# One written order over the whole kernel, a first chunk in halves, and key subtraction one step ahead

## The chip, the cores and the metric

The kernel runs on one core of one Trainium2 chip. A core has five engines that run beside each other, each with its own instruction queue taken in order: TensorE (PE in the profile, with its weight loads shown as PEld), VectorE (DVE), ScalarE (ACT), GpSimd (POOL) and SyncE (SP), which here issues all the transfers. The metric is the device time of one execution in microseconds (us); lower is better.

## What is computed

One transformer layer in float32, on x of shape 2 x 2048 x 256: attention with compressed queries and keys and rotary parts, then a gated feed-forward part.

```python
h = layernorm(x)
kv_c = h @ W_kv;  kv_c = kv_c * rsqrt(mean(kv_c * kv_c) + 1e-6) * g_kv     # 256 -> 64
q_c = h @ W_q                                                               # 256 -> 128
k = concat(heads(kv_c @ W_kdec, 16), rope(heads(h @ W_krope, 32)))          # 16 heads of 48
q = concat(heads(q_c @ W_qdec, 16), rope(heads(q_c @ W_qrope, 32)))
v = heads(kv_c @ W_vdec, 16)
x = x + (softmax(causal(q @ k.T / sqrt(48))) @ v) @ W_o
h = layernorm(x)
x = x + (silu(h @ Wg.T) * (h @ Wu.T)) @ Wd.T      # integer weights times 1/127, hidden size 768
```

## The kernel before

**Tiling.** Each batch of 2048 tokens is cut in four chunks of 512 (`CH`), so there are eight chunks or groups `(b, g)`. The 16 heads are taken four at a time (`u` from 0 to 3). A step of the attention is `(b, u, g)`: four heads, one chunk of queries, all chunks of keys up to `g`. There are 32 steps.

**Part 1, projections.** For each chunk a chain of jobs runs: `measure` (layer-norm moments on DVE, the inverse root on POOL), `norm` (scaling on DVE), `turn` (eight PE transposes and one ACT copy to `xln`), `compressed` (the `kvq` matmuls, L252 and L255, then ACT copies to `qc` and `kv` and a mean of squares on DVE and POOL), `kv_norm` (ACT), `kv_turn` (PE transposes, ACT). Then `project_jobs` makes keys and queries: `k_0`, `k_1` (`rp_k`, L298, eight PE instructions each) and `q_0`, `q_1` (`rp_q`, L301); each is followed by two DVE multiplications from PSUM with the cosine and sine tables (`tcos`, `tsin`, L306), two POOL additions (L308, L309) and a store to DRAM. `q_content`, `k_content` and `v` follow (L319, L335) with ACT copies. All PSUM tiles of this part come from one ring of four, `two`. The chains of chunks `i+1` and `i+2` are woven between the projections of chunk `i`. The `tcos` tiles are a ring of three, and the raw weights `w_kr_raw` (two) and `w_qh_raw` are staged in that same ring first; `rope_columns` picks columns out of them on ACT.

**Part 2, attention.** Keys and queries are loaded back by head (`load_k`, four steps ahead; `load_q`, two steps ahead). `from_first` subtracts the first key of the batch from all keys, in place, on DVE (L140, L141). In each step, for each 128 keys, `st` matmuls (L535) give scores, ACT takes the exponential (L540), POOL clears the masked triangle in the step's own last chunk (L547), and `acc` matmuls (L561) sum the values, one chunk of keys late. The `st` tiles are a ring of three (`big`). `loads(i)` at the head of a step also issues slices of other work: weight pieces of the feed-forward part, and for the first groups `packed` (loads of attention output and sums), `inverted` (reciprocal on DVE, and a way through DRAM) and `divided`. A table `early` puts the first groups' `projected`, `added`, `measured`, `normed` and `normalized` between the last steps.

**Part 3, feed-forward.** For each group, six times `hidden` (`gu` matmuls, L692, then silu on ACT, a product on DVE, and a split in two halves on ACT and POOL), and between them jobs of the groups that follow: `measured`, `divided`, `packed` after the first, `finished` (L720) of the group before, `normed`, `inverted`, `projected` (`ps_o`, L459) and `added` (L465) after the second, `normalized` (`tp_f`, L499 to L501) and the load of x after the fourth. The `gu`, `ps_o`, `tp_f` and `d` tiles share the ring `big`.

**Order.** Each of the three parts stands in its own block of `tc.manual_schedule(engines=order)`: inside it every engine runs its instructions in the order in which they are written. On an engine, an instruction that waits holds all that are written behind it.

Of the kernel before, what the change touches and what calls it, by code (L numbers as in the profile page):

```python
# [9 lines left out]
FP = mybir.dt.float32  # L10
# [8 lines left out]
P = 128  # L19
# [21 lines left out]
def block_kernel(ctx: ExitStack, tc: tile.TileContext, x, w_kv, g_kv, w_kc, w_v, w_q, w_qh, w_kr, w_o,  # L41
# [25 lines left out]
    def inverse_sqrt(dst, src, eps):  # L67

        nc.gpsimd.tensor_scalar_add(dst, src, eps)
        nc.gpsimd.tensor_tensor(dst, dst, neg_half, ALU.pow)  # L70

    def moments(src, name):

        stats = small.tile([P, NT, 6], FP, tag="stats", name=f"stats_{name}")
        mv = small.tile([P, NT, 2], FP, tag="mv", name=f"mv_{name}")
        rstd = small.tile([P, NT], FP, tag="rstd", name=f"rstd_{name}")
        for t in range(NT):
            nc.vector.bn_stats(out=stats[:, t, :], in_=src[:, t, :])
        for t in range(NT):
            nc.vector.bn_aggr(out=mv[:, t, :], in_=stats[:, t, :])  # L80
        inverse_sqrt(rstd, mv[:, :, 1], LN_EPS)
        return mv, rstd

    def scaled(dst, src, mv, rstd):
        for t in range(NT):
# [61 lines left out]


    with ExitStack() as actx:
# [8 lines left out]
        actx.enter_context(tc.manual_schedule(engines=order))  # L158
        xt = {(0, 0): load_x(prep, 0, 0, bufs=3)}
# [6 lines left out]
        def staged(src, shape, name):  # L166
            w = rope.tile(shape, FP, tag="tcos" if shape[0] == P else "done", bufs=3 if shape[0] == P else 2, name=name)
# [3 lines left out]
        w_kr_raw = [staged(w_kr[d * P:(d + 1) * P, :], [P, NH * 64], f"w_kr_raw_{d}") for d in range(2)]  # L171
        w_kv_sb = weight(w_kv, [P, 2, KVR], "w_kv_sb", True)
        w_q_sb = weight(w_q, [P, 2, QR], "w_q_sb", True)

# [42 lines left out]
        for d in range(2):  # L217
            rope_columns(w_kr_sb[:, d, :], w_kr_raw[d])
# [66 lines left out]
        def project_jobs(b, g):  # L285
# [3 lines left out]
            def rope_job(e, k):  # L289

                def job():
# [11 lines left out]
                    tcos = rope.tile([P, 2, CH], FP, tag="tcos", bufs=3, name=f"tcos_{name}")  # L303
# [51 lines left out]
        for k in (measure, norm, turn):  # L355
            job(0, k)
        job(1, measure)

        first_loads = ([(load_k, step) for step in steps[:NC]] + [(load_q, step) for step in steps[:AHEAD]]
                       + [(from_first, step) for step in steps[:NC]])  # L360
# [6 lines left out]
        for i, one in enumerate(chunks):  # L367
# [3 lines left out]
            k_0()  # L371
            if i == 0:

                job(1, norm)
                columns()
                job(0, compressed)
                k_1()
                job(1, turn)
                job(0, kv_norm)
                job(2, measure)  # L380
                q_0()
                job(0, kv_turn)
                q_1()
                job(1, compressed)
            else:
                job(i + 2, measure)
# [99 lines left out]
    def normed(b, g):  # L486

        of, xns[b, g] = xns[b, g], taken([P, NT, C], FP, tag="xn", name=f"xn_f_{b}_{g}")
        scaled(xns[b, g], x1[b, g], *of)
# [14 lines left out]
    with ExitStack() as actx:  # L504
# [76 lines left out]
        def loads(i):  # L581
# [13 lines left out]
            if 0 <= j < 3:  # L595
# [34 lines left out]
        with tc.manual_schedule(engines=order):  # L630

            end = len(steps) - 1
            early = {(end - 2, 1, 0): (projected, added), (end - 2, 1, 2): (measured,), (end - 1, 0, 2): (normed,),
                     (end - 1, 1, 0): (normalized,), (end - 1, 2, 0): (projected, added)}
            waiting = []
            for i, step in enumerate(steps):
                loads(i)
                by_chunk = exp_jobs(*step)
                for c, (jobs, values) in enumerate(by_chunk):
                    for k, job in enumerate(jobs):  # L640
                        job()
                        if k == 0 and waiting:
                            waiting.pop()()
                        if c == 0 and k == 3 and NC - 1 < i + NC - 1 < len(steps):
                            from_first(*steps[i + NC - 1])
                        if k in (0, 2):
                            for one in early.get((i, c, k), ()):
                                one(*groups[0 if i < len(steps) - 2 or c < 2 else 1])
                    waiting.append(values)
            waiting.pop()()  # L650
# [83 lines left out]
    with tc.manual_schedule(engines=order):  # L734
        x1[groups[2]] = load_x(fp, *groups[2], bufs=4)
        for i, one in enumerate(groups):
            parts[one] = split("hT_%d_%d" % one, [P, NF, CH])
            for f in range(NF):
                hidden(*one, f)
                if f == 0:  # L740
                    if i + 1 < len(groups):
                        measured(*groups[i + 1])
                    if 2 < i + 2 < len(groups):
                        divided(*groups[i + 2])
                    if i + 3 < len(groups):
                        packed(*groups[i + 3])
                if f == 1:
                    if i:
                        finished(*groups[i - 1])
                    if i + 1 < len(groups):  # L750
                        normed(*groups[i + 1])
                    if i + 3 < len(groups):
                        inverted(*groups[i + 3])
                    if i + 2 < len(groups):
                        projected(*groups[i + 2])
                        added(*groups[i + 2])
                if f == 3:
# [204 lines left out]
```

## Time and profile before

| what | value |
|---|---|
| median of 3 runs | 1095.1 us (1094.64 to 1097.89) |
| the profiled execution's own time | 1096.71 us |
| its span, first to last instruction | 1095.0 us |
| PE busy | 1066.9 us (97%), 6657 matmul instructions |
| ACT busy | 654.5 us (60%) |
| DVE busy | 310.0 us (28%) |
| POOL busy | 281.2 us (26%) |
| moved by DMA | 93.25 MB, mean 85 GB/s |

Part 1 takes the first 177 us of the span, attention the stretch from 177 to 922 us, and the feed-forward part the rest. A busy time is a sum over the whole span, while each part has its own limits. The granted clock of PE is listed by stretch: 1.00 is full speed and 0.50 is half. The float32 matmuls appear as two PE instructions each. Spans in the tables are in us from the first instruction; in a row of groups the time in square brackets is the engine's idle time just before, with what ended it.

### The profile page before, as it was taken

The numbers are of one execution on the slowest core, as the hardware profiler recorded it, in microseconds if no ns is written. First come the engines' busy times: TensorE is split into PE (matmuls) and PEld (weight loads), VectorE is DVE, ScalarE is ACT, GpSimd is POOL, SyncE is SP. The second block draws the span as 40 slices with busy tenths as digits, with TensorE's granted clock in tenths as the row PEclk, the third lists the DMA queues.
The fourth block names the chain that finished last, engine by engine and source line by source line (L and its number), as shares of the span: only waits on it lengthen the run. The fifth ranks groups of instructions, "written<-read, shape, count | busy, mean of one in ns | idle before, by whom it ended". The sixth has DMA issues, their size and how long they took to land.

```text
span 1095.0 us, 16796 instructions
## 1 busy us (share of the span) xinstructions
PE 1066.9 (97%) x6657; PEld 536.8 (49%) x6657; DVE 310.0 (28%) x454; ACT 654.5 (60%) x816; POOL 281.2 (26%) x377
## 2 busy tenths in 40 slices
PE   6999998999999999999999999999999999899997
PEld 3455544444433433444344344444435445788886
DVE  4677793200210210120011121003001101656552
ACT  2343344777777677777777767767776675343242
POOL 2666764111110210211121031021111001455343
PEclk9999999999999999999999999999999999999999
DMA  8556746110610421311031033122101001242201
GB/s 192 167 210 203 251 139 217 56 39 23 182 55 13 135 75 61 92 54 39 20 104 53 31 98 98 40 78 80 39 14 36 11 10 43 89 131 87 79 20 43
DMA packets 54440, 93.25 MB, mean 85 GB/s; under 512 B 9296, under 2 KB 22992, under 8 KB 54352
## 3 DMA queue, kind: packets, MB, share of 16 engines
q1 hardware_dynamic: 54352, 92.09, 27.3%
q8 instruction: 54, 0.88, 0.4%
q14 instruction: 34, 0.28, 0.1%
HBM read 49.09 MB, written 42.98 MB: 84 GB/s over the span
## 4 chain that ended last, share of the span: by engine, by line
PE 91%; DMA 4%; POOL 2%; DVE 1%; SPq 1%; issue 1%; ACT 0%; DVEq 0%; ACTq 0%; POOLq 0%
PE st L535 45%; PE acc L561 22%; PE gu L692 8%; PE d L720 4%; PE rp_k L298 3%; PE ps_o L459 3%; PE rp_q L301 2%; DMA x<-in_x_dram 2%; DMA kc<-cont_k 1%; DMA w_qh_raw<-in_w_qh_dram 1%; PE kvq L255 1%; PE kvq L252 1%; PE tp_f L499 1%; PE cp_q L319 1%; PE cp_k L319 1%
## 5 line engine op out<-in xcount | busy, mean ns | idle before, releaser
L540 ACT ACTIVATE es<-st 128x1024 f32<-128x1024 f32 (+1 forms) x576 | 513.2, 995 | 172.4 <-PE st L535 171.8
L535 PE MATMUL st<-qT,kT 48*128 48x512 f32 (+3 forms) x2560 | 496.8, 537 | 3.5 <-issue 3.0
L535 PEld LDWEIGHTS st<-qT,kT 48*128 48x128 f32 x2560 | 228.6, 186 | 251.2 <-ACT es L540 117.8
L547 POOL TENSOR_SCALAR_AFFINE_SELECT es<-es 128x256 f32<-128x256 f32 (+1 forms) x192 | 96.3, 510 | 644.2 <-ACT es L540 644.0
L561 PE MATMUL acc<-es,v_sb 128*32 128x512 f32 (+3 forms) x2560 | 250.5, 531 | 0.0
L561 PEld LDWEIGHTS acc<-es,v_sb 128*32 128x32 f32 x2560 | 74.8, 109 | 183.5 <-issue 145.4
L141 DVE TENSOR_TENSOR kT<-kT,k 48x1024 f32<-48x1024 f32 x64 | 81.8, 1279 | 155.1 <-DMA kT<-kc 108.4
L695 ACT ACTIVATE silu<-gu 128x512 f32<-128x512 f32 x48 | 28.6, 598 | 94.3 <-PE gu L692 94.3
L704 POOL TENSOR_TENSOR hT_lo<-h,hT_hi 128x512 fp32r<-128x512 f32 x48 | 61.7, 1287 | 77.3 <-ACT hT_hi L703 77.3
L298 PE MATMUL rp_k<-xln,w_kr_sb 128*128 128x512 f32 x128 | 61.1, 622 | 1.1 <-ACT xln L98 1.1
L699 DVE SCALAR_TENSOR_TENSOR h<-gu,silu 128x512 f32<-128x512 f32 x48 | 33.0, 689 | 83.8 <-ACT silu L695 58.5
L720 PE MATMUL d<-w_d,hT_lo 128*128 128x256 f32 x192 | 46.4, 283 | 0.0
L720 PE MATMUL d<-w_d,hT_hi 128*128 128x256 f32 x192 | 46.4, 283 | 0.0
L569 ACT COPY at<-acc 128x512 f32<-128x512 f32 x32 | 18.7, 585 | 38.9 <-PE acc L561 35.3
L692 PE MATMUL gu<-x_f_hi,w_g 128*128 128x512 f32 x96 | 40.0, 417 | 0.2 <-DVE h L699 0.2
L298 PEld LDWEIGHTS rp_k<-xln,w_kr_sb 128*128 128x128 f32 x128 | 24.2, 198 | 29.4 <-issue 27.6
L692 PE MATMUL gu<-x_f_lo,w_g 128*128 128x512 f32 x96 | 38.0, 396 | 0.0
L692 PE MATMUL gu<-x_f_hi,w_u 128*128 128x512 f32 x96 | 37.6, 392 | 0.0
L692 PE MATMUL gu<-x_f_lo,w_u 128*128 128x512 f32 x96 | 37.4, 390 | 0.0
L720 PEld LDWEIGHTS d<-w_d,hT_lo 128*128 128x128 f32 x192 | 36.8, 192 | 0.3
L720 PEld LDWEIGHTS d<-w_d,hT_hi 128*128 128x128 f32 x192 | 36.8, 192 | 0.3
L258 ACT COPY qc<-kvq 128x512 f32<-128x512 f32 x8 | 4.7, 586 | 44.5 <-PE kvq L255 44.5
(94 smaller groups left out, 744.1 us busy)
## 6 DMA issues: line engine op xcount, KB each, us to landing
x<-in_x_dram SPq DMA_DIRECT2D x16, 512.0 KB
kr<-tcos_k SPq DMA_DIRECT2D x16, 512.0 KB
qr<-tcos_q SPq DMA_DIRECT2D x16, 512.0 KB
kT<-kr SPq DMA_DIRECT2D x64, 128.0 KB
qT<-qr SPq DMA_DIRECT2D x64, 128.0 KB
ad<-at SPq DMA_DIRECT2D x32, 256.0 KB
vd<-v_sb SPq DMA_DIRECT2D x8, 574.0 KB
qc<-cont_q SPq DMA_DIRECT2D x8, 512.0 KB
```

The costliest lines, as they stand in the source:

```text
L141: nc.vector.tensor_tensor(t[rows], t[rows], k0[b, u][rows].unsqueeze(2).to_broadcast([DIM, 2, CH]), ALU.subtract)
L298: nc.tensor.matmul(ps[:, s, :], lhsT=w_kr_sb[:, d, cols], rhs=xln[b, g][:, d, :], start=(d == 0), stop=(d == 1))
L459: nc.tensor.matmul(ps[:, t * C:(t + 1) * C], lhsT=attn[b, g][:, d, t * P:(t + 1) * P], rhs=w_o_sb[:, d, :], start=(d == 0), stop=(d == 1))
L535: nc.tensor.matmul(ps[:, a, i * w:(i + 1) * w], lhsT=kT[b, u, c][rows, r, j * P:(j + 1) * P], rhs=qT[b, u, g][rows, r, off:], start=True, ...
L540: nc.scalar.activation(e[:, :, :used], ps[:, :, :used], AF.Exp, scale=SCALE)
L547: nc.gpsimd.affine_select(out=block, in_=block, compare_op=ALU.is_ge, fill=0.0, base=0, pattern=pattern, channel_multiplier=-1)
L561: nc.tensor.matmul(acc[b, u, g][r0:r0 + 32, off:], lhsT=vv[b, c][:, j, h * VW:h * VW + 32], rhs=es[kt, p][:, a], start=(kt == 0), stop=(kt ...
L692: nc.tensor.matmul(ps[:, k, :], lhsT=w[:, d, cols], rhs=x2[b, g][s][:, d, :], start=(d == 0 and s == 0), stop=(d == 1 and s == 1))
L695: nc.scalar.activation(s, ps[:, 0, :], AF.Silu, scale=WS)
L699: nc.vector.scalar_tensor_tensor(h, ps[:, 1, :], WS, s, ALU.mult, ALU.mult)
L704: nc.gpsimd.tensor_tensor(lo, h, hi.bitcast(FP), ALU.subtract)
L720: nc.tensor.matmul(ps[t], lhsT=parts[b, g][s][:, f, t * P:(t + 1) * P], rhs=w_d[:, f, :], start=(f == 0 and s == 0), stop=(f == NF - 1 and ...
```

## The change

**Order.** One block of `manual_schedule` (`written`) covers all three parts, from the first load to the last store, in place of three.

**Start.** x of the first chunk comes in two loads of two tiles each. Moments, scaling, transposes and copies of the first chunk are done by halves (moments of both halves, then scaling of both). `w_kv` and `w_q` are loaded ahead of `w_kr_raw`, the `tcos` ring has four buffers, and `rope_columns` of `w_kr` stands behind the copies of `xln`. PE transposes the identity 26 times before the first chunk's transposes, and four times after them, into a PSUM tile `warm` that nobody reads; it is the first of the ring `two`. In chunk 0 the jobs run in the order `compressed(0)`, `k_0`, `measure(1)`, `columns`, `k_1`, `norm(1)`, `kv_norm(0)`, `q_0`, `kv_turn(0)`, `q_1`, `measure(2)`, `turn(1)`, `compressed(1)`.

**Subtraction.** Part 1 holds `from_first` of step 0 alone, one place later than before; each step of the attention then has `from_first` of the next step behind its second tile of keys. Before, the first four stood in part 1 and each step had that of the third step ahead behind its fourth tile.

**Before the feed-forward part.** `packed` of group 3 moves to step 27 of the attention, `measured` and `normed` of group 1 to the last step (with a tile of its own in `xpool`), and in part 3 `packed` runs four groups ahead instead of three.

The diff, without the lines that only move to the left with the blocks:

```diff
-        actx.enter_context(tc.manual_schedule(engines=order))
-        xt = {(0, 0): load_x(prep, 0, 0, bufs=3)}
+        written.enter_context(tc.manual_schedule(engines=order))
+        xt = {(0, 0): prep.tile([P, NT, C], FP, tag="x", bufs=3, name="x_0_0")}
+        halves = [slice(i * NT // 2, (i + 1) * NT // 2) for i in range(2)]
+        for half in halves:
+            nc.sync.dma_start(out=xt[0, 0][:, half],
+                              in_=x[0, half.start * P:half.stop * P, :].rearrange("(t p) d -> p t d", p=P))
...
-            w = rope.tile(shape, FP, tag="tcos" if shape[0] == P else "done", bufs=3 if shape[0] == P else 2, name=name)
+            w = rope.tile(shape, FP, tag="tcos" if shape[0] == P else "done", bufs=4 if shape[0] == P else 2, name=name)
...
-        w_kr_raw = [staged(w_kr[d * P:(d + 1) * P, :], [P, NH * 64], f"w_kr_raw_{d}") for d in range(2)]
         w_kv_sb = weight(w_kv, [P, 2, KVR], "w_kv_sb", True)
         w_q_sb = weight(w_q, [P, 2, QR], "w_q_sb", True)
+        w_kr_raw = [staged(w_kr[d * P:(d + 1) * P, :], [P, NH * 64], f"w_kr_raw_{d}") for d in range(2)]
...
-        for k in (measure, norm, turn):
-            job(0, k)
-        job(1, measure)
+        warm = two("warm")
+        def turn_unit(times):
+            for _ in range(times):
+                nc.tensor.transpose(warm[:, 0, :P], ident, ident)
+
+        turn_unit(26)
+        xn = prep.tile([P, NT, C], FP, tag="xn", name="xn_0_0")
+        xln[0, 0] = prep.tile([P, 2, CH], FP, tag="xln", name="xln_0_0")
+        of = [moments(xt[0, 0][:, half], f"0_0_{i}") for i, half in enumerate(halves)]
+        tp = two("tp_0_0")
+        for half, one in zip(halves, of):
+            scaled(xn[:, half], xt[0, 0][:, half], *one)
+        for half in halves:
+            for t in range(half.start, half.stop):
+                for d in range(2):
+                    nc.tensor.transpose(tp[:, d, t * P:(t + 1) * P], xn[:, t, d * P:(d + 1) * P], ident)
+            cols = slice(half.start * P, half.stop * P)
+            nc.scalar.copy(xln[0, 0][:, :, cols], tp[:, :, cols])
+        turn_unit(4)
+        for d in range(2):
+            rope_columns(w_kr_sb[:, d, :], w_kr_raw[d])
 
         first_loads = ([(load_k, step) for step in steps[:NC]] + [(load_q, step) for step in steps[:AHEAD]]
-                       + [(from_first, step) for step in steps[:NC]])
+                       + 2 * [(lambda *step: None, steps[0])] + [(from_first, steps[0])])
...
-            k_0()
             if i == 0:
-                job(1, norm)
-                columns()
-                job(0, compressed)
-                k_1()
-                job(1, turn)
+                job(0, compressed)
+                k_0()
+                job(1, measure)
+                columns()
+                k_1()
+                job(1, norm)
                 job(0, kv_norm)
-                job(2, measure)
                 q_0()
                 job(0, kv_turn)
                 q_1()
+                job(2, measure)
+                job(1, turn)
                 job(1, compressed)
             else:
+                k_0()
...
-            if 0 <= j < 3:
+            if 0 <= j < 3 or (j, k) == (3, 0):
                 (packed, inverted, divided)[k](0, j)
...
-            early = {(end - 2, 1, 0): (projected, added), (end - 2, 1, 2): (measured,), (end - 1, 0, 2): (normed,),
-                     (end - 1, 1, 0): (normalized,), (end - 1, 2, 0): (projected, added)}
+        early = {(end - 2, 1, 0): ((projected, 0), (added, 0)), (end - 2, 1, 2): ((measured, 0),),
+                 (end - 1, 0, 2): ((normed, 0),), (end - 1, 1, 0): ((normalized, 0),),
+                 (end - 1, 2, 0): ((projected, 1), (added, 1)), (end, 0, 2): ((measured, 1),),
+                 (end, 1, 2): ((normed, 1),)}
...
-                        if c == 0 and k == 3 and NC - 1 < i + NC - 1 < len(steps):
-                            from_first(*steps[i + NC - 1])
+                    if c == 0 and k == 1 and i + 1 < len(steps):
+                        from_first(*steps[i + 1])
...
-                    if i + 1 < len(groups):
-                        measured(*groups[i + 1])
+                if 0 < i < len(groups) - 1:
+                    measured(*groups[i + 1])
...
-                    if i + 3 < len(groups):
-                        packed(*groups[i + 3])
+                if i + 4 < len(groups):
+                    packed(*groups[i + 4])
...
-                    if i + 1 < len(groups):
-                        normed(*groups[i + 1])
+                if 0 < i < len(groups) - 1:
+                    normed(*groups[i + 1])
...
+    written.close()
```

`moments` and `scaled` take the number of tiles from their source instead of always four; nothing else in them changes.

## The prediction

> **What bounds the kernel now.** I read the page's busy times and its chain first, then PE's waits, then the granted clock by stretch, then the timeline at each place where PE waits. The page:
>
> ```profile
> PE 1066.9 (97%) x6657; PEld 536.8 (49%) x6657; DVE 310.0 (28%) x454; ACT 654.5 (60%) x816; POOL 281.2 (26%) x377
> ...
> PE 91%; DMA 4%; POOL 2%; DVE 1%; SPq 1%; issue 1%; ACT 0%; DVEq 0%; ACTq 0%; POOLq 0%
> ```
>
> PE ends the chain nearly everywhere, and from 180 to 830 us it is busy 100% of every stretch at clock 1.00. The change takes no matmul out and adds 30 transposes, so time can only come from PE's idle 28 us and from what PE does at half clock. The waits of PE (engine, line, who released it: us in total, times, longest):
>
> ```profile
> PE tp L97 <- DVE xn L86: 9.0, 1, 9.0
> PE st L535 <- issue: 3.0, 1, 3.0
> PE tp_f L499 <- DVE x L465: 2.8, 1, 2.8
> PE cp_k L319 <- DVE tsin_q L306: 2.7, 1, 2.7
> PE ktp L279 <- ACT kvn L272: 1.6, 1, 1.6
> PE rp_k L298 <- ACT xln L98: 1.1, 1, 1.1
> ```
>
> Each occurs once: at the start (9.0, 1.1), in chunk 0 (2.7), at the end of the projections (1.6), at the first score (3.0), in the first feed-forward group (2.8). The last 7 us after PE's end are untouched. Now the clock, in stretches of 3.41 us (columns: busy us of PE, PEld, DVE, ACT, POOL, then PEclk, DMA share, GB/s):
>
> ```profile
> 38.33:41.74 3.41, 2.88 (x10) 1.83 (x12) 3.41 (x6) 0.77 (x1) 2.89 (x3) 0.50 0.02 5
> ...
> 161.20:164.62 3.42, 2.16 (x7) 1.16 (x8) 3.18 (x3) 1.97 (x5) 3.19 (x3) 1.00 0.61 211
> 174.87:178.28 3.41, 1.05 (x5) 0.85 (x7) 2.25 (x2) 0.59 (x1) 1.08 (x1) 1.00 0.58 202
> 178.28:181.70 3.42, 3.42 (x13) 2.70 (x11) 0.00 (x0) 2.25 (x3) 2.35 (x6) 0.50 0.36 139
> ...
> 936.06:939.47 3.41, 3.41 (x13) 3.00 (x12) 1.68 (x3) 1.64 (x2) 1.27 (x1) 0.50 0.27 95
> 11.03:14.44 3.41, 2.31 (x5) 0.97 (x4) 0.00 (x0) 1.01 (x1) 0.00 (x0) 1.00 0.96 188
> ```
>
> The clock falls to 0.50 for exactly one such stretch after each long wait, and all edges lie on one grid of 3.41 us. A stretch with 1.05 us of PE work was followed by a slow one, one with 2.16 us was not. At the start the column says 1.00, but the eight `rp_k` instructions took 6.21 us there (12.44 to 18.65) against 3.43 later (22.16 to 25.59): PE began slow, stayed so after a stretch with 2.31 us of work, and ran fast from 17.85, after a full one. The three later slow stretches cost half of their PE time: 1.44, 1.71 and 1.70 us.
>
> What ends the three middle waits, from the timeline (start, duration, engine):
>
> ```profile
> 34.79 1.40 DVE L78 BATCH_NORM_STATS2 stats<-x 128x6 f32<-128x256 f32 x4 [6.64 <-DMA x<-in_x_dram]
> ...
> 174.77 1.22 DVE L306 TENSOR_TENSOR tcos_q<-rp_q,cos 128x1024 f32<-128x1024 f32 x1 [3.56 <-DMA kr<-tcos_k]
> 175.91 1.21 DVE L306 TENSOR_TENSOR tsin_q<-rp_q,sin 128x1024 f32<-128x1024 f32 x1
> ...
> 934.61 1.15 DVE L465 TENSOR_TENSOR x<-ps_o,x 128x1024 f32<-128x1024 f32 x1
> ...
> 935.82 1.79 PE L499 MATMUL tp_f<-ident,xn_f 128*128 128x128 f32 x8 [2.75 <-DVE x L465]
> ```
>
> In chunk 0 DVE stands at `measure(2)` for chunk 2's x, ahead of `q_0`'s multiplications. At the end of part 1 it stands for a `tcos` buffer, and the first score starts at 177.22, right after `tsin_q` (177.12). In the first group `added(2)` stands behind `measured(1)` and `normed(1)`.
>
> **Start.** Before, the first real matmul starts at 12.44. Full x landed at 5.41. I take 4.5 and 5.2 for the halves (earlier than 3.5 the queues had hardly moved anything; 5.4 is the old time). DVE: four statistics take 1.41 and four aggregates 0.36, so both halves' moments end near 6.2. POOL's pair of operations took 7.18 to 8.54, 1.4 each time, now twice: 5.4 to 6.85 and 6.85 to 8.2. Scaling two tiles is 0.7: the second half ends at 8.9, its transposes at 9.2, ACT's half copy (0.59 by the `qc` row of that shape) at 9.8. First matmul 9.85: **2.6 us** sooner (0 to 3.5). The second pair on POOL eats part of the halving.
>
> 26 transposes at the slow pitch (eight took 1.44 us from 935.82 to the next start; I take 0.2 each) last 5.2 us from 1.5, where `ident` is ready. A stretch with 2.88 us of work was enough at 38.33, and for five of six positions of the grid one such lies inside, so `kvq` and `k_0` run at full speed: 6.21 − 3.43 = **2.8 us** (1.0 if PE slows down again before 9.8). They delay no transposes: xn arrives after their end. `rope_columns` (four copies of 0.36) end near 11.3, under `kvq`'s 3.5 us, so `k_0` isn't late although `w_kr_raw` (landed by 8.1) now follows 192 KB of other weights.
>
> Chunk 0 after that: `kvq` 9.85, `k_0` 13.4, `k_1` 16.85 to 20.3, `q_0`, `ktp`, `q_1` to 24.3 (1.72, 0.6, 1.72). `w_qh` landed at 17.2 before and its copies end before 20.3, so no wait. But DVE now does `k_0` (two of 1.15), `measure(1)` (1.8) and `k_1` (2.3) before `norm(1)`: it begins at 23.4 and shares its stretch with POOL's additions, where it took 3.36 before. So xn of chunk 1 is ready near 26.3, and `turn(1)` waits 2 us. `kvq(1)` needs `q_0`'s PSUM buffer, read by DVE until 28.6: almost 2 us more. Then `kvq`, `cp_q`, `cp_k`, `v` (3.5 + 1.75 + 1.0 + 1.0) end at 35.9; these two waits lie together and most grid positions slow PE once (0 to 1.7, taken 1.1): 37.0 against 42.20. The old wait for x at 34.8 leaves PE, but `kv_norm(1)` and `norm(2)` are behind it on DVE and forbid much more. Start in all: **5.2 us** (2 to 9.8, the last without any wait).
>
> **End of part 1.** `from_first` of steps 1 to 3 leaves the projections. At 149.99 and 155.99 two pairs took 3.70 and 3.42 on DVE, and POOL's additions beside them 2.25 instead of 1.27. That delay reaches `ms`, `kvn`, and PE's 1.6 us wait. What stays, step 0's, moves to chunk 6 with about 4 us and 3 us of DVE slack in a chunk (15.7 busy of 19). Chunk 6 took 19.40 against 18.95 for the others (0.45); chunk 7 lost 1.57 and 0.44 of `ktp` pacing. Sum 2.4. The fourth `tcos` buffer and the freed DVE end the 3.56 wait, so `tsin_q` ends before `v`. Next is ACT's copy of `v` out of PSUM: `warm` shifts the ring by one, so the first score tile lies over `v`'s buffer; 1.02 plus starts makes 1.3 us instead of 3.05: 1.75. A wait of 1.3 leaves over 2 us of work in any stretch, so no slow one: 1.7. Against this, the subtractions of steps 1 to 3 (six of 1.22 to 2.33) now run during the first step beside POOL's last additions and first masks: −0.5 (0 to −2). **5.4 us** (2.5 to 6).
>
> The Trainium skill, "SBUF — State Buffer", section "SBUF: two separate sides", says that of DVE and GpSimd the loser of their shared port blocks for the whole instruction. By that rule POOL could be held for up to six subtractions, 7.3 us, which would, as an estimate, take about 3 us from this term; the 2.25 us additions show roughly one extra us each, not a full block.
>
> **Attention.** Each step's subtraction is the same two instructions. Written two steps later, it stands behind the weight conversions and `divided`, which wait for transfers issued a step before; who waits for it is the score of the step's own chunk `g`. In the tightest case (g = 1) that is a whole chunk (7.07 + 3.57 us) into the step, and the load was issued four steps earlier. Cost 0 (0 to 1).
>
> **First group.** `measured(1)` and `normed(1)` (1.76 + 1.4 us of DVE, 1.3 of POOL) go under the last step, where DVE is idle from 879.2 to 927; POOL's stand ahead of that step's own masks, which begin only at its last chunk. `packed(3)` goes to step 27, three transfers behind which only loads with two steps' lead stand. `added(2)` can then follow `ps_o` at 929.4 if x of group 2 (issued 925.04) has landed; its transfers end by 932.3, so it ends between 930.7 and 933.5, against `gu`'s end at 932.95. The idle 2.75 and the slow stretch's 1.70 go: **4.4 us** (3 to 4.5).
>
> **Sum.** 5.2 + 5.4 + 4.4 = 15.0. The span becomes 1095.0 − 15.0 = 1080.0; the profiled execution is 1.7 longer than its span, and the median 1.6 shorter than that execution, so the median is again the span within 0.1: **1080 us**.
>
> The skill's "TensorE: Matmul & The Clock Gate", section "HAM oscillation", asks for idle gaps beyond 3.4 us before the clock falls; the gaps here are 2.69, 3.05 and 2.75 and it fell each time. By the rule nothing would be won from the clock at the last two places, and the sum would be 11.6; the measured 0.50 decides.
>
> **Rivals.**
> *Chunk 0 gives the gain back.* DVE's new order (`measure(1)`, `norm(1)` behind two key jobs) and the load of chunk 2 hold PE, or PE slows down again: the start gives 1 to 2. Against: even then the first matmul is earlier. 1084 (1082 to 1088).
> *No waits at all in chunk 0.* PE work from 9.85 is 22.5 us, ending at 32.4: 9.8 there, 1075.5. Against: xn(1) and x(2).
> *Single order does nothing and the ring doesn't help:* first score still ends with DVE, chunks 6 and 7 improve only. Total 11.5, 1083.5; inside the first rival's range.
> *Slower: subtractions too late.* If PE stood at chunk `g` for the two subtractions (2.44 us) in each of the 28 steps that remain after the first four, it would cost 68 us: 1148. It turns the sign when steps lose over 0.54 us on average. It needs DVE to be held by a transfer for a whole chunk; the longest in the trace is landing a few us into a step.
>
> **Chances.** Forecast 0.62 (1076 to 1083), gain given back 0.2, no waits 0.1, slower 0.05; 0.03 for no difference. About 0.3%, 3.3 us, is what a measurement of this kernel can tell. Faster 0.92, same 0.03, slower 0.05. Range 1074 to 1088.
>
> **What would show it.** The second half's copy near 9.8 and `kvq` ahead of `rp_k`; PE's waits at `tp` L97 twice, near 2 us, in place of `cp_k`; first score near 168 with about 1.3 us before it, no 0.50 stretch behind it; no wait at `tp_f` L499; attention at 100%. Wrong would be a `st` wait on `kT` in the attention, or a first matmul later than 12.

## The result and the profile after

The changed kernel ran in 1085.33 us (median of 6 runs, 1081.98 to 1087.19) against 1095.95 us (6 runs, 1094.64 to 1097.89) for the kernel before on the same chip: a ratio of 0.9896, with a 95% interval from 0.9876 to 0.9916. The profiled execution took 1085.72 us, its span is 1083.9. That is 11.1 us off the span of before, where 15.0 were forecast.

The page of the changed kernel, busy times and the shares of the chain:

```profile
PE 1066.2 (98%) x6687; PEld 536.8 (50%) x6687; DVE 309.8 (29%) x454; ACT 653.9 (60%) x817; POOL 282.0 (26%) x379
...
PE 82%; DVE 1%; POOL 0%; ACT 0%; issue 0%; DVEq 0%; ACTq 0%
```

PE has 30 instructions more and is busy 0.7 us less: the extra transposes are paid back by matmuls that no longer run at half clock. Its waits (engine, line, releaser: us in total, times, longest):

```profile
PE ktp L285 <- ACT kvn L278: 3.3, 1, 3.3
...
PE st L564 <- ACT v_sb L348: 1.2, 1, 1.2
PE kvq L258 <- ACT xln L99: 1.1, 1, 1.1
PE tp L98 <- DVE xn L87: 0.9, 1, 0.9
...
PE acc L590 <- POOL es L576: 0.7, 1, 0.7
```

The 9.0 at the start, the 2.7 at `cp_k`, the 3.0 at the first `st` and the 2.8 at `tp_f` are gone. Three waits that the forecast didn't have are new in place or size: 3.3 at `ktp`, 0.7 at `acc`, and 0.75 at the first `rp_q`, for ACT's copy to `w_qr_sb`; the forecast had said "so no wait" there, and the second profile has none.

Each landmark of PE's timeline (in us, `k_0` and `k_1` are the starts of `rp_k`) shows where the two kernels draw apart. The third row is the changed kernel profiled again beside the experiments, the last one the fastest variant below.

| | k_0 chunk 0 | k_0 chunk 1 | k_1 chunk 1 | k_0 chunk 2 | k_0 chunk 6 | k_0 chunk 7 | first `st` | first `gu` of the feed-forward part | span |
|---|---|---|---|---|---|---|---|---|---|
| before | 12.44 | 42.20 | 49.58 | 61.97 | 137.79 | 157.19 | 177.22 | 922.05 | 1095.0 |
| changed | 12.38 | 34.91 | 47.25 | 59.65 | 135.47 | 154.42 | 170.28 | 915.72 | 1083.9 |
| changed, again | 12.85 | 38.53 | 45.10 | 57.49 | 133.31 | 152.26 | 168.12 | 913.53 | 1082.0 |
| clock held, chunk 1 | 12.33 | 34.88 | 41.45 | 53.84 | 129.66 | 148.62 | 164.47 | 909.91 | 1078.1 |

Between chunk 1's `k_1` and chunk 6's `k_0` all four rows move in step (88.2 us each), so the start is decided before 50 us. The gain by stage, with the end of part 1 counted up to the second step's first full row of scores (187.61 before, 180.10 after, 177.93 in the second profile):

| stage | forecast | changed | changed, again |
|---|---|---|---|
| start, to chunk 6 | 5.2 | 2.3 | 4.5 |
| end of part 1 with the first step | 5.4 | 5.2 | 5.2 |
| attention | 0 | −1.2 | −1.2 |
| feed-forward part | 4.4 | 4.8 | 4.5 |
| sum | 15.0 | 11.1 | 13.0 |

**The start, twice.** In the first profile chunk 1's `k_0` starts at 34.91, earlier than the forecast 37.0, and then PE stands:

```profile
41.94 1.21 PE L285 MATMUL ktp<-ident,kvn 128*128 128x128 f32 x4 [3.33 <-ACT kvn L278]
...
45.55 1.88 PE L98 MATMUL tp<-ident,xn 128*128 128x128 f32 x8
```

Behind the wait the clock falls (0.50 from 43.8 to 47.3): the eight transposes at 45.55 take 1.88, where the run with the clock held needs 1.04. DVE shows why PE stood: it waits for x of chunk 2, and the mean of squares `ms` that `kvn` needs is written behind the moments of that x.

```profile
36.86 1.40 DVE L79 BATCH_NORM_STATS2 stats<-x 128x6 f32<-128x256 f32 x4 [6.68 <-DMA x<-in_x_dram]
...
38.46 0.39 DVE L270 TENSOR_REDUCE ms<-sq 128x4 f32<-128x256 f32 x1
```

The second profile of the same program has no wait at `ktp`. There PE ran at half clock earlier, and x of chunk 2 (at 35.09) was hidden behind that. Its granted clock by stretch (PE, PEld, DVE, ACT, POOL busy, then PEclk, DMA share, GB/s):

```profile
24.33:27.74 3.41, 1.09 (x6) 0.67 (x6) 3.41 (x4) 0.76 (x1) 1.64 (x2) 1.00 0.93 149
27.74:31.15 3.41, 3.11 (x15) 3.11 (x15) 2.90 (x3) 0.25 (x1) 2.63 (x3) 0.50 0.91 274
31.15:34.56 3.41, 3.41 (x7) 1.81 (x7) 0.00 (x0) 0.00 (x0) 2.32 (x2) 0.50 0.72 225
```

Three short waits (0.93 and 0.94 at `tp`, 1.10 at `kvq`) fell for the most part into the first of these stretches, which left 1.09 us of work in it, and two slow stretches followed. In the first profile `rp_q` had waited 0.75 earlier, `tp` stood only once, and an edge of the grid at 26.78 (five stretches before the fall at 43.84) cut through the wait at `kvq`: 2.16 and 2.62 us of work were left in the two stretches, and the clock stayed at 1.00 up to 43.8.

**The end of part 1** is as drawn: no slow stretch, and `st` waits for the copy of `v` alone.

```profile
170.28 6.74 PE L564 MATMUL st<-qT,kT 48*128 48x512 f32 x40 [1.21 <-ACT v_sb L348]
```

**The attention** lost time in a place that the forecast had not looked at. Here are DVE, POOL and PE while PE is in step 29:

```profile
839.83 2.76 DVE L142 TENSOR_TENSOR kT<-kT,k 48x1024 f32<-48x1024 f32 x2
```

```profile
840.58 0.93 POOL L576 TENSOR_SCALAR_AFFINE_SELECT es<-es 128x512 f32<-128x512 f32 x1 [0.78 <-ACT es L569]
841.49 1.19 POOL L69 TENSOR_SCALAR rstd_f<-mv_f 128x4 f32<-128x4 f32 x1
```

```profile
844.47 0.43 PE L590 MATMUL acc<-es,v_sb 128*32 128x128 f32 x8 [0.70 <-POOL es L576]
```

The subtraction for step 31, now written at the head of step 30 and so right behind `measured(0)` on DVE, runs beside one of step 29's masks on POOL and the addition ahead of its inverse root (0.93 and 1.19 here, 0.64 and 0.23 with the subtraction elsewhere, below). POOL's next mask stands behind these, and `acc` waits for it.

**The first feed-forward group** has no wait at `tp_f` left; `added(2)` runs at 924.19, before `tp_f`:

```profile
924.19 1.22 DVE L491 TENSOR_TENSOR x<-ps_o,x 128x1024 f32<-128x1024 f32 x1 [1.47 <-DMA x<-in_x_dram]
...
926.58 1.03 PE L528 MATMUL tp_f<-ident,xn_f 128*128 128x128 f32 x8
```

### The profile page after: what moved, and what is told of

The parts are those of the page before. It is cut to its first block, busy times and chain, and to the rows that moved or that the text cites. A ratio compares the mean times of both kernels' runs of the same rounds, so it can differ in the third digit from the quotient of the medians.

```text
span 1083.9 us, 16862 instructions
## 1 busy us (share of the span) xinstructions
PE 1066.2 (98%) x6687; PEld 536.8 (50%) x6687; DVE 309.8 (29%) x454; ACT 653.9 (60%) x817; POOL 282.0 (26%) x379
## 4 chain that ended last, share of the span: by engine, by line
PE 82%; DVE 1%; POOL 0%; ACT 0%; issue 0%; DVEq 0%; ACTq 0%
PE st L564 45%; PE acc L590 22%; PE gu L722 8%; PE d L750 4%; PE ps_o L485 3%; PE tp_f L528 1%; POOL es L576 0%; DVE h L729 0%; DVE small_ones L696 0%; DVE x_f_lo L530 0%; POOL rstd_f L69 0%; POOL rstd_f L70 0%; ACT es L569 0%; ACT x_f_hi L529 0%; DVE y L757 0%
## 5 line engine op out<-in xcount | busy, mean ns | idle before, releaser
L564 PEld LDWEIGHTS st<-qT,kT 48*128 48x128 f32 x2560 | 226.0, 186 | 250.8 <-ACT es L569 119.7
L304 PE MATMUL rp_k<-xln,w_kr_sb 128*128 128x512 f32 x128 | 58.1, 598 | 0.0
L462 DVE RECIPROCAL rec<-all_sums 128x64 f32<-128x64 f32 x8 | 4.4, 548 | 160.4 <-DMA all_sums<-ad 160.4
L722 PE MATMUL gu<-x_f_hi,w_g 128*128 128x512 f32 x96 | 39.4, 411 | 0.2 <-DVE h L729 0.2
L491 DVE TENSOR_TENSOR x<-ps_o,x 128x1024 f32<-128x1024 f32 x8 | 9.8, 1225 | 101.2 <-PE ps_o L485 99.7
```

Source lines behind the costliest of these rows:

```text
L304: nc.tensor.matmul(ps[:, s, :], lhsT=w_kr_sb[:, d, cols], rhs=xln[b, g][:, d, :], start=(d == 0), stop=(d == 1))
L564: nc.tensor.matmul(ps[:, a, i * w:(i + 1) * w], lhsT=kT[b, u, c][rows, r, j * P:(j + 1) * P], rhs=qT[b, u, g][rows, r, off:], start=True, ...
L722: nc.tensor.matmul(ps[:, k, :], lhsT=w[:, d, cols], rhs=x2[b, g][s][:, d, :], start=(d == 0 and s == 0), stop=(d == 1 and s == 1))
```

## The experiments

Two theories for the start stood against each other. The first: the load of chunk 2's x takes back whatever chunk 0 gains, because DVE stands at the moments of that x. The second: the clock is lost in the short waits of chunk 1's chain. Other runs take single parts of the change out again. Spans are compared with the 1082.0 of the changed kernel's second profile, medians with its 1083.80. The runs were made on three chips: the first four below, the next four, and the last four. The kernel before ran there in 1096.27, 1095.51 and 1095.82 us, so under 1 us between groups shows nothing.

**The changed kernel again, and with the moments of chunk 2 written behind `compressed(1)`.** The first is the reference, the second takes the load of x out of the chain:

```diff
-                job(2, measure)
                 job(1, turn)
                 job(1, compressed)
+                job(2, measure)
```

> The changed kernel again, for the same chip as the three others. Median near 1085 us, 10 to 11 us under the kernel before. What is looked at: when the statistics of chunk 2's x begin on VectorE (36.86 us in the first profile, 34.79 in the kernel before), how long TensorE then waits for the key transposes of chunk 1 (3.3 us), and whether a half-clock stretch follows.

> The moments of chunk 2 stand behind the compressed job of chunk 1, otherwise the changed kernel. Theory A (VectorE stands for chunk 2's x in front of the mean squares of chunk 1, so the key transposes of chunk 1 wait, and the wait also drops the clock): the wait of 3.3 us and the slow stretch of 1.7 us go, a wait of about 1 us may come at the transposes of chunk 2, so 3.5 to 5 us faster than the changed kernel. Theory B (VectorE is late with chunk 1 anyway, because its own moments and scaling now stand behind two key jobs): the wait stays near 3 us and the time within 1 us.

Measured: 1083.80 us (1082.77 to 1084.04), ratio 0.9889 [0.9871, 0.9906], and 1083.63 us, ratio 0.9886 [0.9868, 0.9904]. No difference: PE was at half clock from 27.7 to 34.6 us in the first (two stretches) and from 25.3 to 35.6 in the second (three), and the x of chunk 2 arrived under it. The load isn't what these runs lose. It isn't theory B either: neither profile has a wait at `ktp`.

**One transposition in place of 26 and 4.**

```diff
-        turn_unit(26)
+        turn_unit(1)
...
-        turn_unit(4)
```

> One transposition of the identity instead of 26 and none of the four, so that the ring of PSUM tiles stays as it is. The first kvq and rp_k matmuls should run at half clock again and chunk 1's first key job start 2.5 to 3 us later. Theory A: the key transposes of chunk 1 stay where chunk 2's x puts them (near 42 us), so the total stays within 1 us of the changed kernel: the warm clock was given back. Theory B (the terms of the start add up): 2.5 to 3 us slower than the changed kernel.

Measured: 1087.60 us, ratio 0.9922 [0.9909, 0.9936], 3.8 us slower than with the transposes. PE's timeline in chunk 0, without them:

```profile
8.93 3.51 PE L258 MATMUL kvq<-w_kv_sb,xln 128*128 128x64 f32 x16
...
15.61 7.03 PE L304 MATMUL rp_k<-xln,w_kr_sb 128*128 128x512 f32 x16
```

and with them, in the changed kernel's first profile:

```profile
8.88 1.90 PE L258 MATMUL kvq<-w_kv_sb,xln 128*128 128x64 f32 x16
...
12.38 7.03 PE L304 MATMUL rp_k<-xln,w_kr_sb 128*128 128x512 f32 x16
```

`kvq` starts no later with the turning than without it (8.88 against 8.93), and by `k_0` it gives 3.2 us, or 2.8 against the 12.85 of the second profile, as forecast. The gain is not taken back later: chunk 2's `k_0` is 4.0 us late (61.48 against 57.49). The 1.2 us beyond the 2.8 are a third stretch at half clock in chunk 1 (29.1 to 39.4), where the second profile has two. Whether it comes from the missing transposes or from the place of the grid was not tested; the run with the moments moved has three with the transposes.

**The first feed-forward group as before** (`packed` three groups ahead, `measured` and `normed` of group 1 in part 3).

```diff
-            if 0 <= j < 3 or (j, k) == (3, 0):
+            if 0 <= j < 3:
...
-                 (end - 1, 2, 0): ((projected, 1), (added, 1)), (end, 0, 2): ((measured, 1),),
-                 (end, 1, 2): ((normed, 1),)}
+                 (end - 1, 2, 0): ((projected, 1), (added, 1))}
...
-                if 0 < i < len(groups) - 1:
+                if i + 1 < len(groups):
                     measured(*groups[i + 1])
```

> packed, measured and normed of the first feed-forward groups stand where they stood before; all else is the changed kernel. If that part is worth what its own wait and slow stretch cost (2.75 + 1.70 us), 4.4 us slower than the changed kernel, with the wait at the transposes of group 1 back. A rival says that x of group 2 and not the order on VectorE ends that wait: then under 2 us.

Measured: 1087.69 us, ratio 0.9927 [0.9913, 0.9941], 3.9 us slower. The wait is back, 3.19 us at `tp_f` for `x` L491, and the `gu` matmuls after it run at half clock (0.63 each up to 931, 0.40 later). The forecast had 4.4.

**The clock held in chunk 1's waits**: the moments of chunk 2 behind `compressed(1)` as above, and transposes of the identity that nobody reads, twelve before `turn(1)`, eight within it, eight before `compressed(1)`.

```diff
+                    for _ in range(12):
+                        nc.tensor.transpose(tp[:, 1, 3 * P:], ident, ident)
...
+                            if (d, t) == (0, 3):
+                                for _ in range(8):
+                                    nc.tensor.transpose(tp[:, 1, 3 * P:], ident, ident)
...
+                    for _ in range(8):
+                        nc.tensor.transpose(ps[:, 1, :P], ident, ident)
```

> The kernel with the moments of chunk 2 later, and TensorE given 28 more transpositions of the identity inside the waits around chunk 1's transposes (12 before them, 8 between the third and the fourth, 8 before the kvq matmuls), each into PSUM columns that the real work overwrites. Theory C (what the start lost is the half clock: the waits for xn of chunk 1 leave so little work in a stretch that the clock falls for two or three stretches, and kvq, cp_q of chunk 1 run at half speed): no stretch at 0.50 between 24 and 36 us, kvq of chunk 1 in 3.6 us instead of 6.9 to 7.0, and the whole 3 to 4.5 us faster than with the moments moved alone (1083.6). Rival D (the waits themselves, or chunk 2's x, hold everything whatever the clock): within 1 us of it.

Measured: 1079.69 us (1079.5 to 1080.19), ratio 0.9855 [0.9837, 0.9872], 4.1 us faster than the 1083.80 of the changed kernel and 3.9 faster than with the moments moved alone. The stretches that were slow in the changed kernel's second profile, here at the same places:

```profile
24.33:27.74 3.41, 3.18 (x28) 2.77 (x26) 3.41 (x4) 1.01 (x1) 1.14 (x1) 1.00 0.91 152
27.74:31.15 3.41, 3.41 (x20) 2.46 (x20) 2.41 (x3) 0.00 (x0) 3.13 (x3) 1.00 0.88 279
```

With 3.18 us of work where 1.09 stood, the clock stays. Chunk 1's `k_0` starts at 34.88 instead of 38.53 (3.65 us), and the span is 3.9 us shorter. Of the 3.65, 0.5 were there before the clock fell: the 26 transposes took 5.36 us here and 5.81 in the second profile, and chunk 0's `k_0` starts at 12.33 instead of 12.85. From chunk 0's `kvq` to chunk 1's `k_0` it takes 26.06 us here and 26.03 in the first profile, both at 1.00; with two slow stretches it takes 29.18 (the second profile), with three 30.40 (the moments moved). So the half clock cost 3.1 or 4.3 us there, and the price that the forecast put on it (1.1) was too small by 2.0 to 3.2.

The loss is the rule and not the exception: of the ten profiles of the changed kernel and its variants that have no such transposes in the waits, nine show the half clock in chunk 1's chain, five of them for two stretches and four for three. Only the first profile stays at 1.00 there, and so do the three with the extra transposes.

**The chain of chunk 1 brought forward** (`measure(1)` before `k_0`, `norm(1)` before `k_1`, no extra transposes).

```diff
                 job(0, compressed)
-                k_0()
                 job(1, measure)
+                k_0()
+                job(1, norm)
                 columns()
                 k_1()
-                job(1, norm)
```

> Moments of chunk 1 ahead of the first key job and its scaling ahead of the second one, moments of chunk 2 later; no further turning. Theory C with the named cause (the scaling stands on VectorE behind two key jobs and beside GpSimd's additions): the two waits of 0.9 us at chunk 1's transposes go, the clock stays up, chunk 1's first key job starts near 33 to 35 us instead of 38.5, and the whole is 3 to 6 us faster than the changed kernel, 1078 to 1081. If only the clock mattered and the order not, the result equals that with the kept turning; if chunk 2's x binds next, a wait at the transposes of chunk 2 of 1 to 3 us appears and the gain is under 2 us.

Measured: 1083.67 us (1082.67 to 1084.53), ratio 0.989 [0.9874, 0.9906]: none of the 3 to 6 us that were expected. `xn` is early, but PE still waits at the same place, for another releaser:

```profile
PE tp L98 <- DVE tsin_k L312: 2.8, 1, 2.8
```

The transposes need a buffer of the ring `two`, and it is the one that `k_1`'s multiplications read. With DVE's work moved ahead of them, they end later. The clock fell again (0.50 from 25.5 to 35.7).

**The subtraction two steps ahead.**

```diff
-                    if c == 0 and k == 1 and i + 1 < len(steps):
-                        from_first(*steps[i + 1])
+                    if c == 0 and k == 1 and i == 0:
+                        from_first(*steps[1])
+                    if c == 0 and k == 1 and i + 2 < len(steps):
+                        from_first(*steps[i + 2])
```

> The subtraction of each step written two steps ahead instead of one (that of step 1 in step 0), otherwise the changed kernel. The last subtraction then no longer stands behind the moments of group 0 on VectorE, where it met GpSimd's masks and rstd at 839.8 us in the profile: the 0.7 us wait of the value matmuls there and its pacing go, 1.2 us faster than the changed kernel. If the meeting is by chance of time and not of order, no difference.

Measured: 1082.79 us (1082.29 to 1083.01), ratio 0.9881 [0.9864, 0.9899]. POOL at the same place:

```profile
838.74 0.64 POOL L576 TENSOR_SCALAR_AFFINE_SELECT es<-es 128x512 f32<-128x512 f32 x1 [0.78 <-ACT es L569]
839.35 0.23 POOL L69 TENSOR_SCALAR rstd_f<-mv_f 128x4 f32<-128x4 f32 x1
```

The wait of `acc` is gone, and that step's piece on PE takes 7.13 instead of 8.03 us. So 0.9 of the 1.2 us that the attention lost were this one overlap of DVE and POOL. The medians alone would not show it: they differ by 1.0 us between two chips.

**The subtractions as before, in the single order** (the first four steps' in part 1, then three steps ahead).

```diff
-                       + 2 * [(lambda *step: None, steps[0])] + [(from_first, steps[0])])
+                       + [(from_first, step) for step in steps[:NC]])
...
-                    if c == 0 and k == 1 and i + 1 < len(steps):
-                        from_first(*steps[i + 1])
+                    if c == 0 and k == 3 and NC - 1 < i + NC - 1 < len(steps):
+                        from_first(*steps[i + NC - 1])
```

> All subtractions as before the change: the first four in the projections, then three steps ahead; all else changed. By the terms of the prediction the end of the projections loses 2 us (VectorE behind, key transposes of chunk 7 late) and the first score comes later by what VectorE is late there; 0.9 us in step 0 and 1.2 us at step 29 come back. In sum 1 to 3 us slower than the changed kernel. Rival: the fourth buffer of the tcos ring alone did it, and the subtraction's place is worth nothing: 2 us faster.

Measured: 1088.75 us, ratio 0.9937 [0.9922, 0.9952], 5.0 us slower than the changed kernel, where 1 to 3 were expected. PE waits in front of chunk 7:

```profile
PE rp_k L304 <- DVE tsin_q L312: 5.0, 1, 5.0
```

The clock falls behind that wait, and the eight instructions take 5.30 instead of 3.70. The move of the subtractions is worth about all of the forecast's term for the end of part 1.

**The whole kernel in three blocks again**, all else as changed.

```diff
+        written.close()
...
+        written.enter_context(tc.manual_schedule(engines=order))
         end = len(steps) - 1
...
         waiting.pop()()
+        written.close()
...
+    written.enter_context(tc.manual_schedule(engines=order))
     x1[groups[2]] = load_x(fp, *groups[2], bufs=4)
```

> The changed kernel with three blocks of written order again instead of one. What differs in the engines' orders: four of step 0's six subtractions come forward between the multiplications of chunk 7 on VectorE, and the loads of the queries of step 2 come forward between chunk 7's stores on SyncE. Theory that the single order is only a notation: 1083.8 (1083 to 1084.6). Theory that it keeps the subtractions of step 0 behind the last multiplications: those of 1.6 to 2 us each stand ahead of chunk 7's multiplications, PSUM comes free late, and 2 to 4 us are lost, 1086 to 1088. A gain is possible too: the first scores' keys are ready earlier, at most the 1.2 us that `st` waits at the end of part 1.

Measured: 1093.54 us (1092.19 to 1094.23, 12 runs), ratio 0.9978 [0.9966, 0.999]: nearly all of the gain is gone. What was expected was too mild, and it named the wrong subtractions: all six of steps 1 to 3, written in the attention, come forward between the multiplications of chunk 6. DVE in this run (the last of step 0's and the first two of the six stand at 144.72, the other four at 150.96):

```profile
144.72 3.61 DVE L142 TENSOR_TENSOR kT<-kT,k 48x1024 f32<-48x1024 f32 x3
...
150.96 6.90 DVE L142 TENSOR_TENSOR kT<-kT,k 48x1024 f32<-48x1024 f32 x4
...
159.03 1.21 DVE L312 TENSOR_TENSOR tsin_q<-rp_q,sin 128x1024 f32<-128x1024 f32 x1
```

and PE:

```profile
160.39 5.09 PE L304 MATMUL rp_k<-xln,w_kr_sb 128*128 128x512 f32 x8 [8.48 <-DVE tsin_q L312]
```

The PSUM buffer of chunk 7's `k_0` comes free at 160.24, after 8.5 us of waiting, and the eight instructions then take 5.09 instead of 3.70. The first score starts at 177.64, against 168.12 and, in the kernel before, 177.22. In this program separate blocks do not keep their instructions apart: subtractions from the head of one block were taken into the block before it.

**The `tcos` ring of three**, all else as changed.

```diff
-            w = rope.tile(shape, FP, tag="tcos" if shape[0] == P else "done", bufs=4 if shape[0] == P else 2, name=name)
+            w = rope.tile(shape, FP, tag="tcos" if shape[0] == P else "done", bufs=3 if shape[0] == P else 2, name=name)
...
-                    tcos = rope.tile([P, 2, CH], FP, tag="tcos", bufs=4, name=f"tcos_{name}")
+                    tcos = rope.tile([P, 2, CH], FP, tag="tcos", bufs=3, name=f"tcos_{name}")
```

> The changed kernel with the `tcos` ring at three buffers again, and nothing else. The forecast gave the wait at the end of part 1 (3.6 of its 5.4 us) to the fourth buffer and the subtractions together. If the buffer carries it: the multiplications of the last chunk wait for a buffer that POOL still reads, and 1 to 4 us come back, 1085 to 1088. If the moved subtractions alone carry it: 1083.8 (1083 to 1084.6). At the start three buffers make the load of `w_qr`'s raw weights no later than the changed kernel does, since it is the third to take one.

Measured: 1088.5 us (1085.93 to 1090.94), ratio 0.993 [0.9906, 0.9954], 4.7 us slower, but not where the expectation looked. From chunk 7's `k_0` to the first score it takes 15.86 us (157.00 to 172.86), just as with four buffers (152.26 to 168.12). The loss is at the start. The fourth cosine product of chunk 0 must wait until the first one has been stored, and PE then waits for its PSUM buffer (chunk 1's `k_0` starts at 41.48 instead of 38.53, its eight instructions take 5.40 instead of 3.70):

```profile
38.00 1.22 DVE L312 TENSOR_TENSOR tcos_q<-rp_q,cos 128x1024 f32<-128x1024 f32 x1 [10.47 <-DMA kr<-tcos_k]
```

```profile
40.41 1.14 PE L341 MATMUL v<-w_v_sb,kvc 64*128 64x256 f32 x8 [3.32 <-DVE tsin_q L312]
```

**The clock held, and the moments of chunk 2 where the change has them.**

> The extra transpositions of the identity are kept, but the moments of chunk 2 stand ahead of `turn(1)` again, as in the changed kernel. Theory x (with the clock held, the load of chunk 2's x is the next limit): its moments hold VectorE until x lands at 35 to 37 us, the squares of chunk 1's latents behind them come late, and the four `ktp` transposes that could start at 38.4 wait 1.7 to 3.3 us, perhaps with a slow stretch behind the wait: 1081.5 to 1084. Theory clock alone (the load matters only in the run that was profiled first): no wait at `ktp`, 1079.7 as with the moments moved.

Measured: 1080.92 us (1080.58 to 1081.95), ratio 0.9865 [0.9843, 0.9888], 1.2 us slower than with the moments moved, between the two theories. In this profile x of chunk 2 was there at 33.38, PE didn't idle at `ktp`, and 0.65 us were lost because the four transposes followed ACT's four `kvn` one by one (1.20 instead of 0.60). The load came at 33.38 in this profile and at 36.86 and 35.09 in the two of the changed kernel, so how much it costs differs from run to run: from 0.65 here to 5.8 in the first profile (`k_1` of chunk 1 at 47.25 against 41.45), there with a slow stretch behind the wait.

**The clock held and the subtraction two steps ahead.**

> Both repairs together: the extra transpositions of the identity in chunk 1's waits with the moments of chunk 2 written behind `compressed(1)`, and the subtraction two steps ahead. If the slow stretches of chunk 0/1 and the late last subtraction are separate losses, their prices add: the kept clock alone ran 1079.7, the two steps alone took 1.0 off, so 1078.7 (1078.0 to 1079.4), with the key projection of chunk 1 at 34.9 us and no wait of `acc` for `es`. Rival: the wait of `acc` depends on where the steps fall and not on the subtraction, then 1079.7 again.

Measured: 1079.62 us (1079.24 to 1079.85), ratio 0.9849 [0.9827, 0.9872]. The wait of `acc` is gone here too and the span is 0.5 us shorter (1077.6 against 1078.1), but the medians are the same within 0.1 us. The expected sum is not shown. This kernel and the one with the clock held alone are the fastest of the study, 4.2 us under the 1083.80 and 5.7 us under the 1085.33 of the changed kernel.

## Why the prediction was right, and where it was off

**The direction and the places were right.** The four long waits of the trace of before ended, and no step of the attention waited for `kT`. The time, 1085.3, is 5.3 above the forecast 1080.0. It is inside the outer range, 1074 to 1088, but not inside the 1076 to 1083 to which the forecast gave 0.62. It lies where the first rival ("chunk 0 gives the gain back", 1082 to 1088, chance 0.2) put it, and by that rival's own sign: the start brought 2.3 in the first profile, near its 1 to 2, although 4.5 in the second.

**The mis-sized term is the start (5.2; measured 2.3 and 4.5).** Its parts:
- First matmul forecast at 9.85, measured 8.88 and 9.35. POOL's pair of operations was priced like that of a whole chunk; a root of two columns takes 0.72 to 0.74 instead of 1.04, and in the first profile the halves' statistics started 0.5 to 0.7 earlier than assumed: the queues, which by the forecast "had hardly moved anything" before 3.5 us, moved 127 GB/s between 2 and 3 us in the trace of before.
- "They delay no transposes: xn arrives after their end" doesn't hold. Without the turning the first real transpose starts 0.47 us after the scaling starts, with it 0.72 (first profile) and 1.29 (second). The real transposes then run faster, which gives part of it back.
- The two waits of chunk 1's chain, forecast as 2 us each, were 0.94 and 1.10 in the first profile, 1.87 together and 1.10 in the second.
- "these two waits lie together and most grid positions slow PE once (0 to 1.7, taken 1.1)" is the step that failed. What its 1.1 stands for is one slow stretch. The waits are shorter than drawn, but behind them stand `kvq`'s sixteen narrow matmuls, and a stretch that they filled (3.11 of 3.41 us) was followed by a second slow one. Where the clock falls it costs 3.1 us for two stretches and 4.3 for three, as the run that holds it shows, not 1.7 at most.
- "The old wait for x at 34.8 leaves PE" holds only where PE is late anyway. Where the clock stayed up, PE arrived at `ktp` at 38.6, before `kvn` (41.49). A cover was assumed that only exists when the other loss occurs: in both profiles of the changed kernel one of the two losses was paid.

**The end of part 1 (5.4; measured 5.2 twice)** was sized right for a partly wrong reason, and so partly by luck. The forecast let two things together end the 3.56 us wait for a `tcos` buffer, the fourth buffer and the freed DVE; the run with three buffers has 0.76 us left of it on DVE and none of it on PE, so the freed DVE was enough without it. The fourth buffer earns its 4.7 us in chunk 0, a place where the forecast gave it nothing. And the forecast took it that the subtractions of steps 1 to 3 leave the projections when they are written later. The three-block run shows that writing them later is not enough: in three blocks they come forward again, and the single order keeps them behind the last multiplications. By the spans that is worth 8.5 us, more than the whole term. The single order was no term of the sum.

**The attention (0, bounds 0 to 1; measured −1.2)** was looked at from the wrong side. The prediction asked who waits for the subtraction's result; nobody does. What it slows is its neighbour POOL, and behind POOL's masks stands `acc`.

**The feed-forward part (4.4; measured 4.8 and 4.5; 3.9 by taking it out)** was right in mechanism and size.

The Trainium skill, "TensorE: Matmul & The Clock Gate", section "HAM oscillation", speaks of idle gaps beyond 3.4 us. Where the clock fell at 27.7 no gap was longer than 1.10 us, and the measurement stands over the rule. What decides in its place stays open. Up to PE's last work, every fall that these profiles show came behind a stretch with at most 1.90 us of PE work. But the first profile has a stretch with 1.60 us (37.01 to 40.43) that no slow one followed, and the next, with 1.90 us (to 43.84), was followed by one, so the work of a single stretch is not the whole rule.

The rule of "SBUF — State Buffer", section "SBUF: two separate sides", that of DVE and GpSimd the one that loses their shared port fully blocks while the other's instruction runs, comes close to what the attention shows. The two subtractions run from 839.83 to 841.01 and from 841.04 to 842.59; POOL's mask starts at 840.58 and its next instruction at 841.49. By that rule, as an estimate, POOL is held for what is left of each subtraction, 0.43 and 1.10 us. The rows show 0.29 and 0.96 more on the two POOL instructions (0.93 against 0.64, 1.19 against 0.23), and 0.33 more on the second subtraction (1.55 against 1.22).

## What to carry to other kernels

Before you count an edit that moves work to a later place as a gain, ask what keeps it there: here, where the order was not written across the boundary, ready work was pulled forward again, ahead of the instruction that PE waited for. Short waits must be added up over one stretch of the clock's grid, and their price counted with what follows them; work that nobody reads, put into those waits, was worth 4 us here, although it takes no wait away. A transfer that is "hidden" behind another loss has to be costed again for the run in which that loss doesn't occur.

## What was not expected of the hardware

A stretch in which PE was busy for 3.11 of 3.41 us, with matmuls of 64 columns, did not bring the clock back. With the moments moved, not even a stretch that was busy throughout, most of it with these (28.73 to 32.14), did. In the kernel before, a stretch with 2.88 us of matmuls of 512 and 256 columns (38.33 to 41.74) did. Why the narrow ones don't count fully was not tested. The grid of the clock lies differently against the same program in each execution (edges at 26.78 and 27.74 in the two profiles of the changed kernel), and nearly the same waits cost nothing in the first and 3.1 us in the second. The six runs of the changed kernel spread over 5.2 us, the four beside the experiments over 1.3, the four with the clock held over 0.7. The load of chunk 2's x, issued at 17.32, 18.37 and 20.36 us in three profiles, let DVE go on at 33.38, 35.09 and 36.86: 16.1 to 16.7 us later, so a delay in issuing it arrived in full in these three.
